# The query product leaves PSUM in one ScalarE copy, and its two parts are made from SBUF by VectorE and POOL

## The chip, the cores and the metric

The kernel runs on one core of one Trainium2 chip. The metric is the device time of one execution in microseconds (us). Before the change the median of three runs is 1530.5 us (1527.78 to 1530.98). A core has five engines that the text names: TensorE (PE in the profile; PEld are its weight loads), VectorE (DVE), ScalarE (ACT), GpSimd (POOL) and SyncE (SP, which here issues DMAs). SBUF is the working memory, and PSUM holds the results of TensorE.

## The reference

The model takes `x` of shape (4, 1024, 256) in float32 and adds four sublayers to it, each behind a layer norm: a linear recurrence over time, a feed-forward part with two top-32 gates, attention, and the feed-forward part again:

```
x = x + lru(layernorm(x));  x = x + ffn(layernorm(x))
x = x + attention(layernorm(x));  x = x + ffn(layernorm(x))
```

The attention has 8 heads of width 64 with a low-rank key and value path. All that matters here is this part of it:

```
q = (x @ Wq.T).reshape(b, t, 8, 64)
latent = x @ Wkv_down.T
k, v = latent @ Wk_up.T, latent @ Wv_up.T
out = softmax(q k^T / 8) v;   return out @ Wo.T
```

Everything is float32 in the reference. The kernel gets close to that by splitting a value into a high part, rounded to the type[...] (`F32R`), and a low part, the value minus its high part.

## The kernel before

**Tiling.** `x` stays in SBUF as 32 tiles of 128 tokens by 256 features, eight for each batch element. In attention the key weights are folded into the query weights (`wqk`, 256 by 512), so that scores are a product of a query with the 64-wide latent. The latent is kept transposed in two parts, `kh` (high) and `kl` (low), each laid down twice, on partitions 0 to 63 and 64 to 127.

**Queries.** `Attention.queries(b, nb, g)` (line 843) makes the queries of a pair of heads `g` (four pairs) for 512 tokens (`nb`, two for each batch element `b`): 32 calls in all. Six matmuls (`products`, line 170) fill a PSUM tile `pmq` of 128 partitions by 512: head 0 of the pair on partitions 0 to 63, head 1 on 64 to 127. The result is a tile `qs` of 128 by 2 by 512: for head `j`, one half of the partitions holds the high part and the other half the low part. The score product then multiplies high and low parts with the latent in one pass, as its contraction runs over all 128 partitions. Lines 852 and 853 make these parts for each `j`: ScalarE copies `pmq` to the half of `qs` named `mine`, rounding it; VectorE subtracts this from `pmq` and writes the half named `other`. So one `pmq` is read four times, twice by each engine. `qs` has two buffers.

**Heads.** `Attention.heads` (line 856) is the main stream. It walks over pairs of heads and query tiles of 128 tokens, and for each head it takes a step: four score matmuls into a PSUM tile `sc` (line 886, two buffers of two banks), the row maximum `nm` on VectorE (line 890), the exponential `pr` on ScalarE (line 894), and then one of two ways of transposing `pr`. Odd query tiles go over TensorE (`ptp`, line 905, copied by ScalarE at line 910). Even ones are cast to two half-precision parts `pd`, the high one on ScalarE (line 897) and the low one on POOL (line 898), and SyncE issues a transposing DMA (line 899). `values_sum` (line 921) multiplies with the latent (`pmo`, line 930), and transposes the reciprocal row sums (`rows`, made by POOL at line 926, line 938), which ScalarE copies to `rb` (line 940) and VectorE multiplies in (line 941). There are 256 steps.

**Side work and its order.** `merge` (line 962) interleaves the main stream with side work: each entry has the step at which it begins. Queries for pair `g` begin seven steps before its first score. The other entries are the output projection (`pmy`), the layer norms and transposes for the next batch element (`pt`, `pml`, `pv`), the head of the second feed-forward part (`pt`, `pc`) and 24 tiles of the first feed-forward part (`pl`, `px`, `pf`, with `ex`, `xg` and `full` behind them). All this side work and `values_sum` take their PSUM tiles in turn from two banks with the tag "s". The order in which the instructions stand on each engine's queue follows this program order, changed by a planner that plays the program through with its own durations (`schedule_with_timeline_sim=True`). On the chip each engine works through its queue in that order.

Of the kernel before, what the change touches and what calls it, by code (L numbers as in the profile page):

```python
# [10 lines left out]
F32 = mybir.dt.float32  # L11
# [5 lines left out]
ALU = mybir.AluOpType  # L17
# [4 lines left out]
P = 128  # L22
# [142 lines left out]
def products(nc, dst, pairs, start=True, stop=True):  # L165


    terms = [(x, y) for a, b in pairs for x, y in ((a[0], b[0]), (a[0], b[1]), (a[1], b[0]))]
    for i, (x, y) in enumerate(terms):
        nc.tensor.matmul(dst, x, y, start=start and i == 0, stop=stop and i == len(terms) - 1)  # L170
# [602 lines left out]
class Attention:  # L773
# [68 lines left out]
    def queries(self, b, nb, g, psum, tag):  # L842

        nc, xnt = self.nc, self.xnt[b, nb]
        qs = self.qs[b, nb, g] = self.wp.tile([P, 2, 512], F32R, tag="qs", name="qs", bufs=2)
        pm = psum.tile([P, 512], tag, "pmq")
        products(
            nc, pm, [([t[:, k, g * P : (g + 1) * P] for t in self.wqk], [t[:, k, :] for t in xnt]) for k in range(KD)]
        )
        for j in range(2):  # L850
            mine, other = slice(j * HD, (j + 1) * HD), slice((1 - j) * HD, (2 - j) * HD)
            nc.scalar.copy(qs[mine, j, :], pm[mine, :])
            nc.vector.tensor_tensor(qs[other, j, :], pm[mine, :], qs[mine, j, :].bitcast(F32), ALU.subtract)  # L853
        yield

    def heads(self, b, psum):
# [468 lines left out]
```

## Time and profile before

| what | value |
|---|---|
| median of the runs | 1530.5 us (1527.78 to 1530.98, three runs) |
| the profiled execution's own time | 1528.76 us |
| its span, first to last instruction | 1527.0 us |
| mean granted clock of TensorE | 0.946 |
| busy over the span: TensorE | 1286.5 us (84%) |
| weight loads | 955.6 us (63%) |
| VectorE | 1184.6 us (78%) |
| ScalarE | 1017.5 us (67%) |
| POOL | 680.3 us (45%) |
| `sc`, first to last start | 376.0 to 1292.0 us |

The profile shows one execution. A group is a set of instructions of one line, one engine and one shape, with its count, its busy time, and the idle time of its engine just before them with what ended it. "A <- B" in a list of waits reads: engine A was idle before that instruction until B was done. Engines overlap, so their busy times don't add up to the span; a wait costs time only where its engine sets the pace.

### The profile page before, as it was taken

How to read it: one execution, taken by the hardware profiler on the slowest of the kernel's cores; microseconds unless marked ns; L12 is line 12 of the kernel's file. 1: busy time of each engine (PE TensorE's matmuls, PEld its weight loads, DVE VectorE, ACT ScalarE, POOL GpSimd, SP SyncE). 2: the span in 40 equal slices, each digit the busy share in tenths (PEclk: the TensorE clock that was granted, in tenths of full speed). 3: DMA queues.
4: the chain of work that ended last, by engine and by line, in shares of the span. 5: the costliest groups of instructions: out<-in, count | busy, mean ns of one | idle time of the engine just before them, and what ended most of it. 6: DMA issues, size and time to landing. Idle time of an engine off the chain costs nothing. (4 is left out here: it accounts for less than half of the span.)

```text
span 1527.0 us, 28727 instructions
## 1 busy us (share of the span) xinstructions
PE 1286.5 (84%) x10134; PEld 955.6 (63%) x10136; DVE 1184.6 (78%) x3682; ACT 1017.5 (67%) x2152; POOL 680.3 (45%) x849
## 2 busy tenths in 40 slices
PE   4879998697898898888998989889999999566675
PEld 3535465376677766766776767677777777334454
DVE  8976665697868887878768687777676675599998
ACT  5353433566887877797777787877777776475674
POOL 2033332161545454544544554454344444067776
PEclk9999999698999999999999999999999999688899
DMA  3110000321454343434433445334344545000000
GB/s 118 32 41 15 21 21 21 128 97 49 84 93 90 61 77 73 77 70 82 82 74 60 72 79 86 61 61 83 68 82 79 92 86 96 1 15 24 22 25 28
DMA packets 288609, 96.51 MB, mean 63 GB/s; under 512 B 268233, under 2 KB 284626, under 8 KB 288466
## 3 DMA queue, kind: packets, MB, share of 16 engines
q1 hardware_dynamic: 283024, 88.50, 28.7%
q10 hardware_dynamic: 5442, 6.18, 1.2%
q8 instruction: 80, 1.31, 0.4%
q14 instruction: 63, 0.52, 0.1%
HBM read 16.01 MB, written 11.53 MB: 18 GB/s over the span
## 5 line engine op out<-in xcount | busy, mean ns | idle before, releaser
L898 POOL TENSOR_TENSOR pd<-pr,pd 128x1024 f16<-128x1024 f32 x128 | 273.5, 2141 | 247.6 <-ACT pd L897 185.7
L890 DVE TENSOR_REDUCE nm<-sc 128x1 f32<-128x1024 f32 x256 | 308.5, 1217 | 78.9 <-PE sc L886 77.5
L894 ACT ACTIVATE pr<-sc,nm 128x1024 f32<-128x1024 f32 x256 | 285.9, 1119 | 84.6 <-DVE nm L892 47.0
L886 PE MATMUL sc<-kh,qs 128*128 128x512 f32 x512 | 184.3, 438 | 26.4 <-ACT pr L894 18.8
L886 PE MATMUL sc<-kl,qs 128*128 128x512 f32 x512 | 162.0, 397 | 0.0
L674 DVE MATCH_REPLACE8 wk<-m,wk 128x256 f32<-128x256 f32 x384 | 154.9, 406 | 0.1
L910 ACT COPY p<-ptp 128x512 f32<-128x512 f32 x224 | 124.1, 590 | 45.3 <-PE ptp L905 33.7
L674 DVE MAX8 m<-wk 128x8 f32<-128x256 f32 x384 | 151.3, 412 | 0.4
L930 PE MATMUL pmo<-p,la 128*64 128x128 f32 x2048 | 144.0, 289 | 6.1 <-ACT ft L524 2.9
L905 PE MATMUL ptp<-ident,pr 128*128 128x128 f32 x1024 | 138.3, 275 | 12.9 <-ACT pr L894 12.4
L930 PEld LDWEIGHTS pmo<-p,la 128*64 128x64 f32 x2048 | 122.8, 144 | 25.0 <-ACT ft L524 5.1
L905 PEld LDWEIGHTS ptp<-ident,pr 128*128 128x128 f32 x1024 | 115.6, 140 | 34.8 <-ACT pr L894 22.2
L897 ACT CAST pd<-pr 128x1024 f16<-128x1024 f32 x128 | 133.5, 1054 | 5.6 <-DMA d<-pd 4.6
L886 PEld LDWEIGHTS sc<-kh,qs 128*128 128x128 f32 x512 | 85.2, 195 | 51.1 <-ACT pr L894 29.8
L886 PEld LDWEIGHTS sc<-kl,qs 128*128 128x128 f32 x512 | 97.0, 190 | 23.2 <-issue 1.4
L930 PE MATMUL pmo<-d,lb 128*64 128x128 f16 x3072 | 103.4, 222 | 7.6 <-DVE qs L853 2.6
L930 PEld LDWEIGHTS <-lb 128*64 128x64 f16 x3072 | 92.2, 111 | 26.3 <-issue 20.1
L628 POOL TENSOR_TENSOR ex<-ex,wk 128x512 f32<-128x512 f32 x61 | 77.6, 1273 | 57.4 <-DVE wk L674 45.5
L926 POOL COPY rows<-rs 128x128 f32<-128x128 f32 x128 | 36.1, 294 | 124.4 <-PE pmo L938 76.3
L941 DVE TENSOR_TENSOR on<-pmo,rb 128x128 f32<-128x128 f32 x128 | 36.4, 285 | 66.8 <-ACT rb L940 66.3
L147 PE MATMUL pt<-ident,xn 128*128 128x128 f32 x256 | 47.8, 309 | 44.5 <-ACT xn L145 32.9
L699 PE MATMUL pf<-wf,vt 128*128 128x256 f32 x288 | 81.2, 427 | 4.6 <-ACT vt L697 4.2
(307 smaller groups left out, 2768.6 us busy)
## 6 DMA issues: line engine op xcount, KB each, us to landing
tt<-ft SPq DMA_DIRECT2D x16, 256.0 KB
tt<-tt SPq DMA_DIRECT2D x8, 512.0 KB
out<-x SPq DMA_DIRECT2D x32, 128.0 KB
x<-in_x ACTq DMA_DIRECT2D x6, 512.0 KB
pf<-pfs SPq DMA_DIRECT2D x12, 256.0 KB
full<-pf SPq DMA_DIRECT2D x24, 128.0 KB
d<-pd SPq DMA_TRANSPOSE x128
wa<-in_w_attn SPq DMA_DIRECT2D x2, 640.0 KB
```

Source lines behind the costliest of these rows:

```text
L147: nc.tensor.transpose(pt[:, k, i * P : (i + 1) * P], xn[:, k * P : (k + 1) * P], ident)
L628: pool.tensor_tensor(ex, ex, wk, ALU.subtract)
L674: ins = make(*args).ins
L699: nc.tensor.matmul(dst, vt[:, k, :], w.wf[:, k, :], start=(k == 0 and bias is None), stop=(k == KD - 1))
L886: nc.tensor.matmul(sc[:, sl], qs[:, j, q * P : (q + 1) * P], kk[:, sl], start=(i == 0), stop=(i == 1))
L890: nc.vector.tensor_reduce(nm, sc, AX.X, ALU.max, negate=True)
L894: nc.scalar.activation(pr, sc, AF.Exp, bias=nm, accum_out=ssum[:, j : j + 1])
L897: nc.scalar.copy(pd[:, 0, :], pr)
L898: nc.gpsimd.tensor_tensor(pd[:, 1, :], pr, pd[:, 0, :], ALU.subtract)
L905: nc.tensor.transpose(pt[:, kk, :], pr[:, kc * P : (kc + 1) * P], self.ident)
L910: nc.scalar.copy(dst, pt)
L930: nc.tensor.matmul(po[j * HD : (j + 1) * HD, 0, :], v, pts[j][:, c, :], start=(n == 0), stop=(n == len(terms) - 1),)
```

## The change

The product is first copied whole, from PSUM to a new SBUF tile `q` of 128 by 512 (one buffer), by one ScalarE instruction. For each head, VectorE then copies `mine` from `q` to `qs`, rounding it, and POOL subtracts that from `q` into the half `other`. So `pmq` is read once, by one engine; both inputs of the subtraction are now in SBUF.

```diff
         products(
             nc, pm, [([t[:, k, g * P : (g + 1) * P] for t in self.wqk], [t[:, k, :] for t in xnt]) for k in range(KD)]
         )
+        q = self.wp.tile([P, 512], F32, tag="q", name="q")
+        nc.scalar.copy(q, pm)
         for j in range(2):
             mine, other = slice(j * HD, (j + 1) * HD), slice((1 - j) * HD, (2 - j) * HD)
-            nc.scalar.copy(qs[mine, j, :], pm[mine, :])
-            nc.vector.tensor_tensor(qs[other, j, :], pm[mine, :], qs[mine, j, :].bitcast(F32), ALU.subtract)
+            nc.vector.tensor_copy(qs[mine, j, :], q[mine, :])
+            nc.gpsimd.tensor_tensor(qs[other, j, :], q[mine, :], qs[mine, j, :].bitcast(F32), ALU.subtract)
         yield
```

## The prediction

> **What bounds the kernel now.** I first read busy time by stretch, to find the stretch that the change lies in. All 64 copies and all 64 subtractions of the query product start between 366 and 1256 us, that is in the attention stage, so the sums below are about this stretch.
>
> ```profile
> core 0: us, PE busy (x) PEld busy (x) DVE busy (x) ACT busy (x) POOL busy (x), PEclk, DMA share, GB/s
> 366.00:376.00 10.00, 7.74 (x36) 6.17 (x35) 5.04 (x17) 4.85 (x11) 1.09 (x2) 0.66 0.00 0
> 376.00:1292.00 916.00, 822.39 (x8245) 655.14 (x8246) 687.13 (x1714) 700.90 (x1366) 428.76 (x420) 0.98 0.42 77
> ```
>
> In these 916 us TensorE is busy for 822 (90%), ACT for 77%, DVE for 75%, POOL for 47%. TensorE sets the pace, and its matmuls are not changed; what can be won or lost is its 94 us of idle time. The waits of TensorE in that window say what the idle time is made of (engine and line, what it waited for, us in total, times, longest):
>
> ```profile
> PE sc L886 <- ACT pr L894: 18.8, 22, 2.8
> PE ptp L905 <- ACT pr L894: 12.4, 16, 1.8
> PE pt L147 <- DVE qs L853: 9.0, 5, 2.1
> PE sc L886 <- DVE qs L853: 6.7, 7, 1.7
> PE pmo L930 <- DVE qs L853: 4.4, 5, 1.6
> ...
> PE pmy L170 <- DVE qs L853: 2.6, 2, 1.3
> ```
>
> Two different waits end with the query's subtraction (L853). `sc` reads `qs`: 6.7 us in 7 waits are true data waits. `pt`, `pmo` and `pmy` read no query at all; they want a PSUM bank. All side work shares the two banks tagged "s", and `pmq` holds one until the last of its four readers is done. That is 9.0 + 4.4 + 2.6 = 16.0 us in 12 waits. One such place in the timeline of ACT and DVE:
>
> ```profile
> 686.02 0.59 ACT L852 CAST qs<-pmq 64x512 fp32r<-64x512 f32 x1
> ...
> 687.33 0.68 DVE L853 TENSOR_TENSOR qs<-pmq,qs 64x512 fp32r<-64x512 f32 x1
> ...
> 688.05 0.58 ACT L852 CAST qs<-pmq 64x512 fp32r<-64x512 f32 x1 [0.86 <-DVE qs L853]
> ...
> 689.22 0.69 DVE L853 TENSOR_TENSOR qs<-pmq,qs 64x512 fp32r<-64x512 f32 x1
> ```
>
> The four readers of the one bank take turns (the second cast sits idle for 0.86 us behind the first subtraction). This product began at 682.59 and left its bank at 689.91, so it held it for 7.3 us. Read the same way for all 32 queries, the hold is 4.9 to 11.1 us, mean 7.8, of which the product itself is about 1.6 and the wait of the first cast for ACT 0.8.
>
> **The change, step by step.** The durations come from these rows of the groups, the first three in the same window, L269 in the set-up at 30 to 60 us (count, busy us, mean ns), and from the view of one line, L636 (min/median/max ns):
>
> ```profile
> L910 ACT COPY p<-ptp 128x512 f32<-128x512 f32 x221 | 122.3, 590 | 41.1 <-PE ptp L905 33.0 <-PE pmo L930 7.3
> L953 POOL TENSOR_TENSOR onp<-on,onp 128x512 fp32r<-128x512 f32 x28 | 35.9, 1280 | 20.3 <-ACT onp L952 16.3 <-DVE m L674 3.1 <-PE ptp L905 0.9
> L908 DVE COPY p<-ptp 128x512 f32<-128x512 f32 x29 | 19.8, 683 | 5.3 <-PE ptp L905 5.0 <-PE pmo L930 0.2
> L269 DVE TENSOR_SCALAR t<-st,cs_s 128x256 f32<-128x256 f32 x1 | 0.3, 339 | 0.0
> ```
>
> ```profile
> L636 DVE SCALAR_TENSOR_TENSOR full<-full,rs,ex x24: 474/864/2319, 402.1 to 1063.7; 128x256 f32<-128x256 f32 x24
> ```
>
> *ACT.* Removed: 64 casts at 0.58 = 37.1 us. Added: 32 copies of 128x512 out of PSUM at 0.59 (L910, the same shape and path) = 18.9. ACT gains 18.2 us.
>
> *DVE.* Removed: 64 subtractions at 0.689 = 44.1 us. Added: 64 copies of 64x512 from SBUF to SBUF. No such row exists. Upper end: L908, 0.68 (it reads PSUM). Lower end: L269 is a one-input float32 pass inside SBUF, 339 ns for 256 columns against 272 for 128, so 0.52 ns per column, and 339 + 256 x 0.52 = 0.47 us for 512. I take 0.45, since the new copy has no per-partition scalar to fetch: 29 us. This rate has a price. L636, a DVE instruction with its inputs in SBUF, takes 0.474 us at best and 2.319 at worst; the worst began at 788.56, while a POOL subtraction of `pd` ran from 788.47 for 2.13 us. The Trainium skill, "SBUF — State Buffer", section "Who interferes with whom", gives the rule, and it speaks against this change: a DVE copy at the double rate takes the port pair that it shares with GpSimd, and whichever issues second is blocked for the whole of the other's instruction. The old subtraction never paid this (0.683 to 0.694 in all 64), as one of its inputs was PSUM. POOL runs 47% of the time, and the remainder of a running POOL instruction, weighted by length, is about 0.8 us (the 2.14 us `pd` dominates), so the rule adds some 0.4 us to each copy: 0.85. By the uncontended row DVE gains 64 x (0.69 - 0.45) = 15 us, by the rule it loses 64 x 0.16 = 10. I take the loss, since L636's median of 864 ns shows the blocking is common here.
>
> *POOL.* Added: 64 subtractions of 64x512. L953 gives 1.28 for 128x512; fewer partitions save nothing (L1035, 32x256, took 0.664, and L659, 128x256, 0.729). What no row shows is that this one writes the other half of the partitions; from 1.28 to twice that, I take 1.28: 82 us, POOL from 47% to 56%.
>
> Now what reaches TensorE:
>
> 1. *The bank.* `pmq` is freed after the one copy: 1.6 + 0.8 + 0.6 = 3.0 us instead of 7.8. The 12 bank waits have a mean of 1.3 us, well under the 4.8 won, so this cause goes; but the other bank or an `xn` of ACT may be next. I take 60% of 16.0: **-10 us** (bounds 0 and -16).
> 2. *The scores.* From the end of the product the shortest chain to the first score was 0.58 + 0.69 = 1.27; it becomes 0.59 + 0.45 + 1.28 = 2.3, so +1.0. This is hidden wherever the first score comes later. In 25 of the 32 queries both subtractions were done 1.6 to 18.7 us before the first score; the first score of the other 7 starts right at the first subtraction's end (688.07 in the query above). If nothing else moves that is 7 x 1.0 = +7. But the queries are late there because the side work ahead of them is held up in the two banks, which step 1 eases. I take **+3** (bounds -6.7, all these waits gone, and +25: 7 x (1.0 + 0.4 + 2.14), each behind a whole `pd` on POOL).
> 3. *ACT's load* falls by 18.2 of 916 us, 2.0 points of its 23 idle ones. Waits of TensorE for ACT are 31 us in the two rows shown and about 44 with the smaller ones; in that proportion (9%) **-4**.
> 4. *DVE's load* rises by 10 us, 1.1 points of 25. It acts mainly through `nm`, for which ACT waits 47.0 + 26.2 us: **+2** by the rule. By the uncontended row alone it would be -2, and the sum below 4 us lower.
> 5. *POOL's queue.* Behind the new subtractions wait `pd` (its DMA result is used several scores later), `ex`, and `rows` (L926), which TensorE transposes at the end of each value sum. By the timeline nine of the 128 `rows` copies are ready less than 1.4 us before that transpose (median 6.2). At a 9% chance (82 of 916 us) of meeting a new subtraction: 9 x 0.09 x 1.3 = **+1**.
>
> The sum is -10 + 3 - 4 + 2 + 1 = -8 us against the profiled execution, which took 1528.8 (span 1527.0 and 1.8 around it): 1521. The three runs shown have a median of 1530.5, 1.7 above it; the same -8 gives 1522.5 there, and between the two I say **1522**.
>
> Nothing covers the new buffer `q`, which has one slot, but the products start at least 12.9 us apart, and the last reader is done some 4 us after the copy.
>
> **The rivals.**
>
> *A. The longer chain decides (slower).* Place: the first scores of 7 queries, which have no slack. Price: up to 3.5 us each. The planner may put the POOL subtractions behind a `pd` that itself waits for ACT (POOL waited 185.7 us for those casts, up to 8.9 at a time), and TensorE, which runs in order, then stands. Gains elsewhere are about 11 net, so it decides from 1.5 us per query; at the full price 1521 - 3 + 25 = 1543. For it: the wait is already there with no slack. Against it: POOL was idle at the moment the new subtraction would start in all 7.
>
> *B. The bank waits only change their name (same).* The 16 us go to the next-late cause and step 1 gives 0: with -4, +3, +2, +1 the result is 1531 to 1532. For it: `pt <- ACT`, `pf <- DVE nm` and others of 1 to 5 us are in the same list. Against it: 4.8 us is large beside a mean wait of 1.3.
>
> *C. The written order comes out worse (slower).* The order on each queue is made by a planner from its own timing of the program, and the start offsets of the side work (6.75, 48.25, -5.5 scores) suit the present order. Batches 1 and 2 repeat each other's slack to 0.01 us in six of eight queries, so a bad place is paid more than once. A score step is 916/256 = 3.6 us; one lost step in each of four batches is 14 us: 1536.
>
> **How the numbers follow.** The forecast has 0.47, A 0.22, B 0.15, C 0.16. About 0.2% (3 us, from 1527.4 to 1533.6) is what a measurement of this kernel can tell from no change. Faster is the forecast alone, 0.47; same is B, 0.15; slower is A and C, 0.38. The likeliest case's own range is 1514 to 1528. The range over all starts where the full 16 us, half of the 6.7 and the 4 are won and steps 4 and 5 cost nothing (16 + 3.4 + 4 = 23, and 1529 - 23 = 1506) and ends at A's full price, **1506 to 1545**.
>
> **What would show it.** In the new profile: no TensorE wait of `pt`, `pmo` or `pmy` on `qs`, and the bank held about 3 us (step 1); `sc` waiting on POOL `qs` for under 10 us in all (step 2; over 20 is A); DVE copies spread from about 0.4 to 2.5 us (the blocking; all at one value means none); POOL subtractions near 1.28; ACT's busy time down by 18. TensorE idle time from other causes grown by as much as `qs` lost is B; many groups of waits changed that have nothing to do with queries is C. The forecast is wrong if the stage's idle time of TensorE, 94 us, doesn't fall.

## The result, and the profile after

The change makes the kernel slightly slower. In 21 runs of each on one chip the median goes from 1528.03 us to 1533.54 us, a ratio of **1.0033 [1.0023, 1.0042]**; a second comparison on another chip gave 1.0030 [1.0019, 1.0041]. The forecast was 1522, faster. The measured time lies within the forecast's range, but the sign is wrong. The profiled execution took 1530.07 us, span 1528.4 us, mean granted clock 0.938.

Busy time of the engines by stretch, kernel after:

```profile
core 0: us, PE busy (x) PEld busy (x) DVE busy (x) ACT busy (x) POOL busy (x), PEclk, DMA share, GB/s
376.00:1292.00 916.00, 822.35 (x8260) 653.63 (x8260) 696.02 (x1718) 682.54 (x1339) 513.46 (x483) 0.98 0.44 78
```

The loads moved as the change says: ACT 700.9 to 682.5, POOL 428.8 to 513.5, DVE 687.1 to 696.0. TensorE is busy as before, 822 of 916 us. So the 94 us of idle time that the forecast wanted to shorten are still there (916.0 less 822.4). The waits of TensorE in the same window, kernel after (engine and line, what it waited for, us in total, times, longest), say what became of them:

```profile
PE ptp L907 <- ACT pr L896: 17.8, 20, 1.8
PE sc L888 <- ACT pr L896: 17.2, 24, 2.2
PE pmq L170 <- DVE on L943: 8.9, 4, 2.3
PE pmo L932 <- DVE on L943: 7.0, 7, 1.9
...
PE pmy L170 <- POOL onp L955: 3.7, 4, 1.0
PE pmo L932 <- ACT q L851: 3.5, 6, 0.9
...
PE pt L147 <- DVE on L943: 3.1, 2, 1.6
...
PE sc L888 <- POOL qs L855: 1.7, 2, 0.8
```

No `pt`, `pmo` or `pmy` waits on `qs` any more: the 16.0 us of bank waits behind the subtraction are gone. Of waits on the query's bank 3.5 us are left, now behind the copy `q` itself. In place of the rest stand waits on `on` (L943, L941 before), the last reader of `pmo`, which holds the other of the two "s" banks. They were 3.9 us before, in four rows of which these are the largest,

```profile
PE pmy L170 <- DVE on L941: 1.5, 1, 1.5
PE pt L147 <- DVE on L941: 1.3, 1, 1.3
```

and are 20.7 us now (the three rows shown and three small ones of 0.9, 0.6 and 0.2): 16.8 came for the 16.0 that went. The second profile of the kernel after has 20.8 us of them, and the kernel with `q` in another pool, below, has 21.1 (the second profile of the kernel before has 3.9).

One such place, among those where the new copies take part. These are lines of the timeline of the kernel after (start, us, engine, instruction, idle time before it and what ended it), around the product that the prediction followed at 682.59 in the kernel before:

```profile
682.45 1.64 PE L170 MATMUL pmq<-xnt,wqk 128*128 128x512 f32 x6
...
687.47 0.62 ACT L851 COPY q<-pmq 128x512 f32<-128x512 f32 x1
...
687.74 2.14 POOL L900 TENSOR_TENSOR pd<-pr,pd 128x1024 f16<-128x1024 f32 x1 [0.64 <-POOL rows L928]
688.14 1.97 PE L932 MATMUL pmo<-p,la 128*64 128x128 f32 x32 [0.33 <-ACT q L851]
688.72 1.90 DVE L854 CAST qs<-q 64x512 fp32r<-64x512 f32 x2
689.53 0.30 ACT L942 COPY rb<-pmo 128x128 f32<-128x128 f32 x1
...
691.84 0.27 DVE L943 TENSOR_TENSOR on<-pmo,rb 128x128 f32<-128x128 f32 x1
692.16 1.53 PE L932 MATMUL pmo<-d,lb 128*64 128x128 f16 x48 [1.79 <-DVE on L943]
```

`pmq` leaves its bank at 688.1 and the next `pmo` follows at once. The one after that needs the other bank. Its `rb` is there at 689.83, but `on` starts only at 691.84, since DVE's queue holds the two query copies and parts of a top-32 gate ahead of it. The two copies take 1.90 us instead of two times 0.40: the first of them started while a POOL `pd` was running and ended just after it. TensorE stands for 1.79 us.

But query copies stand between `rb` and `on` in only four of the 17 waits, 3.9 of the 20.7 us. The five longest, 10.9 us together, are of another kind. One of them, kernel after:

```profile
701.55 4.22 POOL L900 TENSOR_TENSOR pd<-pr,pd 128x1024 f16<-128x1024 f32 x2 [5.03 <-ACT pd L899]
701.57 2.13 DVE L64 SCALAR_TENSOR_TENSOR ax_t<-ax_rs 128x4 f32<-128x4 f32 x1
...
703.74 2.05 DVE L65 TENSOR_TENSOR ax_t<-ax_t,ax_v 128x4 f32<-128x4 f32 x1
...
706.30 0.28 DVE L943 TENSOR_TENSOR on<-pmo,rb 128x128 f32<-128x128 f32 x1
...
706.63 1.65 PE L170 MATMUL pmq<-xnt,wqk 128*128 128x512 f32 x3 [2.23 <-DVE on L943]
```

Here `rb` is ready at 702.58. Ahead of `on` on DVE's queue stand tiny operations of a layer norm, `ax`, which take 0.16 us elsewhere. Two of them start within 0.1 us of the start of a POOL `pd` and take as long as that does. At the same layer norm in the kernel before, `on` stands right behind the first such operation, only one `pd` runs (2.13 us from 701.93), and TensorE does not wait:

```profile
701.96 2.12 DVE L64 SCALAR_TENSOR_TENSOR ax_t<-ax_rs 128x4 f32<-128x4 f32 x1
...
704.01 0.28 DVE L941 TENSOR_TENSOR on<-pmo,rb 128x128 f32<-128x128 f32 x1
```

So most of the waits on `on` come from where the written order puts `on` and `pd`, not from the length of the new copies. That order came with the moved work: with the unused tile alone, below, these waits are 3.7 us. No run moved `on` alone, so what another place for it would give is not shown.

The new operations, from the view of each line, kernel after (ns min/median/max, first and last start):

```profile
L851 ACT COPY q<-pmq x32: 574/586/644, 368.4 to 1249.4; 128x512 f32<-128x512 f32 x32
L854 DVE CAST qs<-q x64: 398/424/2255, 369.0 to 1251.3; 64x512 fp32r<-64x512 f32 x64
L855 POOL TENSOR_TENSOR qs<-q,qs x64: 1258/1310/1461, 370.2 to 1253.0; 64x512 fp32r<-64x512 f32 x64
L636 DVE SCALAR_TENSOR_TENSOR full<-full,rs,ex x24: 476/1060/2431, 404.1 to 1059.1; 128x256 f32<-128x256 f32 x24
```

What is left to explain is the 0.33%. I cut every profile at two places: the end of the last convolution of the first feed-forward part (when ScalarE has read it, 292.6 us in the kernel before), and the first and last score (start of the first, end of the last). "Idle" is the stage's length less TensorE's busy time.

| kernel | convolution to first score | first to last score | of it TensorE idle | last score to end |
|---|---|---|---|---|
| before | 83.5 | 916.4 | 93.6 | 234.6 |
| before, second profile | 83.3 | 914.2 | 92.7 | 236.3 |
| after | 86.9 | 912.3 | 92.5 | 236.9 |
| after, second profile | 87.3 | 917.3 | 93.4 | 235.8 |

Idle time in the attention stage is unchanged. About 3.7 us were lost before the first score, in the mean of two, where only the first query or two had run. The last stretch is about 0.9 us longer in the mean of two, within what the two profiles of one kernel differ by.

### The profile page after: what moved, and what is told of

The parts are those of the page before. It is cut to its first block, busy times and chain, and to the rows that moved or that the text cites. A ratio compares the mean times of both kernels' runs of the same rounds, so it can differ in the third digit from the quotient of the medians.

```text
span 1528.4 us, 28806 instructions
## 1 busy us (share of the span) xinstructions
PE 1291.6 (85%) x10136; PEld 955.6 (63%) x10136; DVE 1194.6 (78%) x3682; ACT 996.0 (65%) x2120; POOL 766.9 (50%) x913
## 4 chain that ended last, share of the span: by engine, by line
PE 43%; DVE 34%; ACT 11%; issue 5%; POOL 4%; DMA 2%; ACTq 0%; POOLq 0%; DVEq 0%
PE pmo L932 8%; PE sc L888 8%; DVE wk L674 7%; DVE nm L892 6%; DVE m L674 5%; PE ptp L907 4%; ACT pr L896 4%; PE po L437 3%; PE pu L170 2%; PE pl L556 2%; PE pmy L170 2%; PE pz L452 1%; DMA d<-pd 1%; PE pfa L567 1%; PE pt L147 1%
## 5 line engine op out<-in xcount | busy, mean ns | idle before, releaser
L932 PE MATMUL pmo<-p,la 128*64 128x128 f32 x2048 | 137.4, 277 | 5.0 <-DVE x L961 1.7
L932 PEld LDWEIGHTS pmo<-p,la 128*64 128x64 f32 x2048 | 115.0, 137 | 26.0 <-issue 7.1
L855 POOL TENSOR_TENSOR qs<-q,qs 64x512 fp32r<-64x512 f32 x64 | 86.6, 1352 | 64.3 <-DVE qs L854 61.5
L699 PE MATMUL pf<-wf,vt 128*128 128x256 f32 x288 | 85.2, 439 | 4.2 <-ACT vt L697 3.7
L556 PE MATMUL pl<-lint,xc_f 128*128 128x512 f32 x128 | 73.3, 660 | 9.8 <-ACT xc_f L587 9.8
```

What stands on the lines that cost most here:

```text
L556: self.last_logits = nc.tensor.matmul(v, x, w.lint, start=False, stop=True).ins
L699: nc.tensor.matmul(dst, vt[:, k, :], w.wf[:, k, :], start=(k == 0 and bias is None), stop=(k == KD - 1))
L855: nc.gpsimd.tensor_tensor(qs[other, j, :], q[mine, :], qs[mine, j, :].bitcast(F32), ALU.subtract)
L932: nc.tensor.matmul(po[j * HD : (j + 1) * HD, 0, :], v, pts[j][:, c, :], start=(n == 0), stop=(n == len(terms) - 1),)
```

## The experiments

### The tile alone

The kernel before with nothing but the allocation of `q`; the tile is never used.

```diff
+        self.wp.tile([P, 512], F32, tag="q", name="q")
```

> The kernel before, with only the tile q allocated and never used: no instruction is added or moved by hand, but the addresses of the attention's tiles shift by 2 KB and the planner writes another order from the end of the first stage on. If the slowdown of 0.33% is the new order that comes with the tile's place: ratio to before 1.002 to 1.005, first score near 379 us instead of 376. If it is the moved work itself: 0.999 to 1.001.

Measured: **1.0032 [1.0021, 1.0043]**, as much as the change loses, without any of its work. The stretch from the convolution to the first score takes 86.1 us. The traces show how an unused tile can do this: the order of the instructions differs from that of before on every engine, from 273 us on for VectorE and from 303 us on for TensorE, and in the attention stage too. (The two profiles of the kernel before have the same order on every engine.) One visible part is the load of the attention weights, `wa`, the view of one tile, first in the kernel before and then with the unused tile:

```profile
L712 SPq DMA_DIRECT2D wa<-in_w_attn x2: 424/726/1029, 294.4 to 294.9; - x2
```

```profile
L712 SPq DMA_DIRECT2D wa<-in_w_attn x2: 430/430/431, 268.5 to 269.0; - x2
```

It is issued 26 us earlier. What is lost before the first score is lost at one place some 60 us after that. Timeline of TensorE and ACT in the kernel before:

```profile
345.30 3.64 ACT L587 ACTIVATE xc_f<-xc_f,bt,bs 128x512 f32<-128x512 f32 x5
348.84 0.45 ACT L650 ACTIVATE ob<-pf,rs 128x256 f32<-128x256 f32 x1
349.19 0.80 ACT L587 ACTIVATE xc_f<-xc_f,bt,bs 128x512 f32<-128x512 f32 x1
349.34 1.99 PE L567 MATMUL pfa<-wf,tt 128*128 128x256 f32 x8 [2.04 <-ACT ob L650]
...
352.78 1.13 PE L567 MATMUL pf<-wf,tt 128*128 128x256 f32 x4 [1.45 <-ACT pfs L581]
354.08 1.03 PE L699 MATMUL pf<-wf,vt 128*128 128x256 f32 x4
```

And with the unused tile:

```profile
348.41 4.34 ACT L587 ACTIVATE xc_f<-xc_f,bt,bs 128x512 f32<-128x512 f32 x6
354.16 1.05 ACT L581 COPY pfs<-pfa 128x512 f32<-128x512 f32 x2
354.78 2.07 PE L567 MATMUL pf<-wf,tt 128*128 128x256 f32 x4 [5.81 <-ACT pfs L581]
356.86 1.91 PE L699 MATMUL pf<-wf,vt 128*128 128x256 f32 x4
356.89 0.47 ACT L650 ACTIVATE ob<-pf,rs 128x256 f32<-128x256 f32 x1
```

Before, a short `ob` stood ahead of the last of six activations on ACT's queue and freed a bank for eight matmuls. Now all six run in one row, followed by a table load, and TensorE waits 5.81 us in one piece instead of 2.04 and 1.45. After that wait the same two groups of four matmuls take 2.07 and 1.91 us instead of 1.13 and 1.03. The windows of the two kernels give the reason, columns as in the first fence, before and then with the tile:

```profile
352.70:356.60 3.90, 3.82 (x19) 3.36 (x20) 3.79 (x16) 2.23 (x6) 1.46 (x2) 1.00 0.35 134
```

```profile
354.70:358.60 3.90, 3.82 (x10) 2.81 (x11) 3.83 (x18) 2.67 (x7) 1.08 (x2) 0.50 0.35 134
```

The granted clock is 0.50 instead of 1.00: in 3.9 us ten matmul records were done instead of 19. The Trainium skill, "TensorE: Matmul & The Clock Gate", Part 1, says that an idle window of about 3.4 us brings TensorE down to half rate; the trace agrees here, where TensorE did nothing in the 3.4 us before the clock fell (350.1 to 353.5). But so long a wait is not needed. In the profile of the last changed kernel below (offset 48.75, `q` in its own pool) the wait of 2.04 us at the same place is followed by half rate, with TensorE busy for 1.36 of the 3.4 us before; columns as above:

```profile
348.70:352.10 3.40, 1.36 (x7) 0.89 (x6) 3.40 (x15) 3.40 (x6) 2.10 (x3) 1.00 0.00 0
352.10:355.50 3.40, 2.77 (x7) 1.76 (x6) 3.40 (x15) 2.88 (x6) 1.26 (x2) 0.51 0.04 16
```

With the unused tile the wait costs 2.3 us more and the half clock 1.8 us more, 4.1 in all, of which 2.7 are left at the first score of this run. All six profiles of kernels with a 2 KB tile in the working pool show this wait of 5.81 us, followed by the two groups at 2.07 to 2.08 and 1.91 us. None of the other twelve has it.

That is not the whole loss of about 4.9 us. In this one profile the stage from the first to the last score is longer too, 921.5 us, with the same idle time (93.3) but 48.2 us at half rate, where the two profiles of the kernel before have 37.5 and 34.3. This execution took 1539.02 us, against a median of 1535.18 for this kernel, so how much of that is usual is not known.

### The change with its tile elsewhere

The whole change, with `q` taken from a pool of its own that is opened ahead of the first feed-forward part.

```diff
+    qpool = ctx.enter_context(tc.tile_pool(name="q_own", bufs=1))
...
+        at.qp = qpool
...
-        q = self.wp.tile([P, 512], F32, tag="q", name="q")
+        q = self.qp.tile([P, 512], F32, tag="q", name="q")
```

> The change, with q in a pool of its own that is opened ahead of the first stage, so that all later tiles shift alike; allocating it there without using it leaves every queue's order as it was before. If the tile's place costs the 0.33%: ratio to before 0.995 to 0.999, as the attention stage itself was 4 us shorter from first to last score in the changed kernel's profile. If the moved work costs it: 1.002 to 1.005, as with the change as made.

Measured: **0.9964 [0.9950, 0.9979]**, faster than before. The convolution-to-score stretch is 82.5 us, with the waits of 2.04 and 1.45 us in it as before. This kernel and the kernel after were then measured once more, on another chip and side by side.

> The change with q in a pool of its own ahead of the first stage, a second time and beside the changed kernel. If the moved work gains in this order: ratio to before 0.995 to 0.998 again, first score near 376 us. If the first result was the chip or chance: 0.999 to 1.002.

> The changed kernel as it is, on the same chip as the next three. If the tile's place and the new order that follows from it cost what the first experiments showed: ratio to before 1.002 to 1.005, and the first score of its profile at 379 us or later.

Measured: 0.9972 [0.9957, 0.9987] and 1.0030 [1.0019, 1.0041]. Where `q` lies is worth 0.6% (1.0030 / 0.9972 = 1.0058) with the same arithmetic on the same engines. Between the two profiles, whose spans differ by 7.0 us, 5.8 lie before the first score (87.3 against 81.5) and 2.2 after the last (235.8 against 233.6); the stage is alike (917.3 and 916.7).

The kernel before was also profiled a second time, to have a measure of how far two profiles of one kernel differ.

> The kernel before, for a second profile of it: first score near 376 us, first to last score 914 to 920 us. A first score at 379 us or later would take the place of the tile out of the explanation.

Measured: 0.9997 [0.9985, 1.0008]; the stage took 914.2 us where it had taken 916.4, with idle times of 92.7 and 93.6.

### Address or order?

An unused tile of half the size at the same place: it moves the addresses of what is allocated after it, but the order of the instructions in the trace is that of before on every engine.

```diff
+        self.wp.tile([P, 256], F32, tag="pad", name="pad")
```

> The kernel before with an unused tile of 1 KB per partition at the place where the change allocates q (half of q's size). It moves the addresses of what is allocated after it, but the order written on every queue stays that of before, instruction for instruction. Theory 'it is the order that the tile redraws which costs': 0.999 to 1.001, first score at 375 to 379 us and about 83 us from the last f1 convolution to the first score. Rival 'the shifted addresses cost by themselves': 1.002 to 1.004 and 86 to 87 us.

Measured: **0.9992 [0.9981, 1.0002]**, 83.8 us to the first score, and `wa` issued at 293.2. Addresses shifted by 1 KB cost nothing, so the loss goes with the order that came with the 2 KB tile; a shift by 2 KB in the old order was not run. Why the planner writes another order for 2 KB and the same for 1 KB is not settled here.

### Is the stage's gain or loss one of a single order?

Two offsets of the side work were moved, to get other written orders of the attention stage. First 6.75 scores for each tile of the first feed-forward part became 6.5, in the kernel before, in the change with `q` in its own pool, and in the change as it is:

```diff
-            start = 1 + 6.75 * n if n < TPB else STEPS * (n // TPB) - STEPS + 48.25 + 8 * (n % TPB + 1)
+            start = 1 + 6.5 * n if n < TPB else STEPS * (n // TPB) - STEPS + 48.25 + 8 * (n % TPB + 1)
```

> The kernel before with the tiles of the first feed-forward part begun every 6.5 steps of the main stream instead of 6.75: the same work, the same addresses, another order from step 20 or so on. As a measure of what an order alone is worth: between 0.997 and 1.006 of before; more likely slower, as 6.75 suits the present order.

> The change with q in its own pool, and 6.5 steps as in o1_b. If the moved work itself gains, whatever the order: 0.2 to 0.6% faster than o1_b. If e4's gain was a lucky order: within 0.1% of o1_b or slower than it.

> The changed kernel, q in the working pool, with the side work's start at 6.5 scores per tile where it was 6.75: the same tile at the same place, the attention stage in another order. Theory 'the loss sits ahead of the first score and the moved work gains little or nothing in the stage': the stretch from the last f1 convolution to the first score is again 86 to 87 us (81.7 with q in its own pool at this offset, 82.9 without q), and the ratio is that of the run with q outside (0.998) plus 0.002 to 0.004: 1.000 to 1.003. Rival 'the loss was an accident of one attention order': 0.997 to 0.999.

Measured: 1.0010 [0.9997, 1.0023], 0.9984 [0.9974, 0.9994] and 1.0022 [1.0012, 1.0032]. With the tile in its own pool the moved work gains 0.26% (0.9984 / 1.0010 = 0.9974); with it in the working pool the stretch before the first score is 87.6 us again, against 81.7, and the gain is lost.

Then the other offset, 48.25, became 48.75, before and with `q` in its own pool.

```diff
-            start = 1 + 6.75 * n if n < TPB else STEPS * (n // TPB) - STEPS + 48.25 + 8 * (n % TPB + 1)
+            start = 1 + 6.75 * n if n < TPB else STEPS * (n // TPB) - STEPS + 48.75 + 8 * (n % TPB + 1)
```

> The kernel before with the offset 48.25 of the later side work at 48.75: another written order of the attention stage, without the change. It is the base for the next run. Either theory: 0.998 to 1.005.

> The change with q in a pool of its own ahead of the first stage, with the same offset at 48.75. Theory 'the moved work is worth 0.2 to 0.4% in any order if the tile stays out of the working pool': 0.996 to 0.998 of the run before it. Rival 'the gain of the two earlier pairs belonged to their orders': 0.999 to 1.003 of it.

Measured: 0.9994 [0.9984, 1.0004] and **0.9933 [0.9915, 0.9951]**: 0.6% between them, more than either theory expected, and the fastest kernel of the study (median 1519.91, six runs). The stage from the first to the last score, in the windows of the two, columns as above, first without and then with the change:

```profile
375.50:1291.80 916.30, 820.39 (x8247) 654.60 (x8248) 688.65 (x1714) 701.03 (x1367) 428.73 (x421) 0.98 0.43 77
```

```profile
378.10:1282.60 904.50, 813.64 (x8245) 646.96 (x8246) 692.26 (x1714) 681.04 (x1335) 513.06 (x482) 0.99 0.45 79
```

Of the 11.8 us, 5.0 are idle time of TensorE (95.9 to 90.9) and 6.8 its busy time: the same matmuls ran faster, since the clock's records show 17.1 us at half rate in the stage instead of 33.9. The waits on `on`, from the list of TensorE's waits of the changed one, are smaller than in the kernel after but still there:

```profile
PE pmq L170 <- DVE on L943: 6.7, 3, 2.3
PE pmo L932 <- DVE on L943: 4.6, 4, 1.8
...
PE pt L147 <- DVE on L943: 3.1, 2, 1.5
```

So with `q` in its own pool the moved work is faster by 0.3% to 0.6% in three written orders. Only in the third do the profiles find the gain in the stage. In the first pair the stage takes 915.8 and 916.7 us with the change, 916.4 and 914.2 without; in the second 916.3 against 916.7. Where those gains lie is not shown, and the waits on `on` are there in all three (21.1, 19.7 and 16.5 us). In the order of the change as it was made the work gains nothing: 1.0033 and 1.0030 stand against 1.0032 for the tile alone.

### Which engine makes which part

Five more kernels free the bank with the one copy, and differ in who makes the high and low parts from `q`. Two have `q` in the working pool.

Low parts on VectorE:

```diff
-            nc.gpsimd.tensor_tensor(qs[other, j, :], q[mine, :], qs[mine, j, :].bitcast(F32), ALU.subtract)
+            nc.vector.tensor_tensor(qs[other, j, :], q[mine, :], qs[mine, j, :].bitcast(F32), ALU.subtract)
```

> The change, with the low parts on VectorE from SBUF and nothing new on POOL. If POOL's 64 new subtractions (82 us) cost the time (longer chain, queue, shared port): 0.997 to 1.000, faster than the change. If VectorE's load does (44 us of subtractions come back beside 27 us of copies, VectorE then near 79% in the stage): 1.005 or more. If it is the order alone: anything from 0.998 to 1.005, with no relation to POOL.

High parts on ScalarE:

```diff
-            nc.vector.tensor_copy(qs[mine, j, :], q[mine, :])
+            nc.scalar.copy(qs[mine, j, :], q[mine, :])
```

> The change, with the high parts made by ScalarE from SBUF, so that VectorE has nothing of the query at all and ScalarE copies three times. If VectorE's copies on the shared port cost the time: 0.997 to 1.000. If ScalarE's load matters more (37 us of casts come back beside 19 us of copies): 1.004 or more. If it is the order alone: anything from 0.998 to 1.005.

Measured: 1.0211 [1.0190, 1.0231] and 1.0001 [0.9992, 1.0010]. The other three have `q` in its own pool: low parts on VectorE, high parts on ScalarE, and both of these edits at once.

> q in its own pool; high and low parts both on VectorE from SBUF, nothing on POOL. If the 2.1% of the second experiment was VectorE's load (27 us added, 37 taken off ScalarE, port waits on the subtractions): 1.012 to 1.022 here too. If it was the tile's place: 0.998 to 1.004.

> q in its own pool; the high parts by ScalarE, the low parts by POOL, nothing on VectorE. If VectorE is what counts in this stage (44 us taken off it): 0.993 to 0.996, faster than the change with q in its own pool. If ScalarE is (19 us added to it, where the change takes 18 off): 0.998 to 1.002.

> q in its own pool ahead of the first stage; one ScalarE copy out of PSUM as in the change, then the high parts by ScalarE and the low parts by VectorE, both from q: the engines of before, 19 us of copies more on ScalarE, nothing on POOL. If freeing the bank after one copy is what gains: ratio to before 0.996 to 0.999. If the gain is VectorE's and ScalarE's relief: 1.001 to 1.006, since ScalarE has more to do.

Measured: 1.0300 [1.0286, 1.0315], 1.0051 [1.0038, 1.0064] and 1.0147 [1.0121, 1.0173]. All three are slower than either theory expected. From first to last score, all with `q` in its own pool:

| high / low parts by | stage, us | ACT busy | DVE busy | POOL busy | TensorE idle |
|---|---|---|---|---|---|
| (kernel before) | 916.4 | 701.3 | 687.4 | 429.1 | 93.6 |
| DVE / POOL (the change) | 915.8 | 682.3 | 696.3 | 513.0 | 92.1 |
| ACT / POOL | 922.3 | 715.3 | 648.5 | 508.2 | 91.9 |
| ACT / DVE | 929.7 | 718.0 | 691.7 | 435.9 | 101.8 |
| DVE / DVE | 957.8 | 683.8 | 725.3 | 434.5 | 116.5 |

The row ACT / DVE is the nearest test of step 1: the same two engines make the same two parts as before, and the bank is freed early, for one more ACT copy per query (ACT +16.7, DVE +4.3). The stage gets 13.3 us longer, in the fastest of the five runs. In TensorE's waits of this kernel no side work waits on `qs`, 1.5 us are left behind the copy `q`, the waits on `on` are 13.5 us, and those for the exponential, which held 31.2 us before, hold 49.0:

```profile
PE sc L888 <- ACT pr L896: 25.9, 32, 2.9
PE ptp L907 <- ACT pr L896: 23.1, 29, 2.3
```

The bank's early release and ACT's added copy can't be told apart in it, and its written order is another one again. In the row DVE / DVE, 38 us more of DVE go with a stage that is 41 us longer. Here the subtraction has both inputs in SBUF, and its spread, from the view of its line, is as wide as the copies' (before, with one input in PSUM, all 64 took 0.683 to 0.694 us):

```profile
L855 DVE TENSOR_TENSOR qs<-q,qs x64: 684/687/2684, 372.4 to 1297.0; 64x512 fp32r<-64x512 f32 x64
```

The working pool is not the worse place for every kernel: DVE / DVE takes 1.0211 with `q` there and 1.0300 outside, and ACT / POOL 1.0001 and 1.0051. The stretch before the first score is longer in both with the tile there (85.0 against 84.3, and 86.9 against 83.2), but the stage is 10.8 and 6.9 us shorter. The tile's place chooses an order; whether that is a good one for the stage has to be measured.

## Why the prediction was wrong

**Step 1, the bank (-10, bounds 0 and -16): this failed.** Its first half holds: the bank is held 3.35 us on average (3.0 expected, 7.8 before), and no side work waits on `qs`. The failed sentence is "this cause goes; but the other bank or an `xn` of ACT may be next. I take 60%". The other bank was next for all of it, 16.8 us on `on` for 16.0 on `qs`. The step gave 0, as in rival B, whose likelihood I had put at 0.15. The mean wait of 1.3 us against 4.8 won was the wrong comparison: side work takes the two banks in turn, so the slack of the other bank's holder had to be compared. `on` waits on DVE, for 3.9 of the 20.7 us behind the copies that the change puts there, and for 10.9 behind operations of a layer norm that last as long as a `pd` on POOL.

**Step 2, the scores (+3, bounds -6.7 and +25).** Better than forecast: true data waits of `sc` on the query fall from 6.7 us in 7 to 1.7 us in 2 waits. The chain got longer (4.5 us on average from the product's end to the first low part, 2.8 before), but the queries came earlier: from the product's start to the first score it is 7.7 us at the least, 4.6 before. Rival A falls.

**Step 3, ACT's load (-4).** The load fell by 20.1 us in the stage (18.2 expected), but TensorE's waits for `pr` rose, 31.2 to 35.0 us. (All its waits for ACT were 48 us before, not 44, which changes the step by less than half a us.) They are not in proportion to ACT's load: `pr` waits for `nm` on DVE. The waits of ACT, kernel after:

```profile
ACT pr L896 <- DVE nm L894: 52.5, 39, 4.2
ACT pr L896 <- DVE nm L892: 39.9, 32, 5.9
```

These held 47.0 and 26.2 us before: ACT's load fell by 20 us, and these waits for DVE grew by 19.

**Step 4, DVE's load (+10 us of load, +2 of time).** The load rose by 7.2 us in the stage, near the value by the rule on the shared port and far from the -15 by the uncontended row. But that is luck: it rose in other instructions than the step said. The copies have a mean of 0.55 us, not 0.85: only 7 of 64 took over 0.75, and 56 ran within 0.45. Their busy time is 34.2 us for 42.7 of subtractions, a gain of 8.5 in the window. What took it back is other DVE work: L636, whose mean went from 972 to 1279 ns (+7.4), and the 18 tiny `ax_t` operations of 128x4 on L65, 3.4 to 13.3 us (+9.9). Five of these 18 take 2.05 us, each beside a `pd` on POOL; one takes 1.14 beside a new subtraction. Of L636, nine take over 1.5 us now and four did before, beside `pd` or `onp` and never beside a new subtraction. So what these met was, but for one, not the added POOL work but old POOL work that the new order puts beside them. The runs show the times, not what they waited for. The price of +2 for this load, together with step 3's -4, was of the wrong sign: +3.8 us in the waits for `pr`.

**Step 5, POOL's queue (+1).** The subtraction takes 1.35 us on average (1.28 expected; writing the other half of the partitions costs nothing that is seen), POOL's load rose by 84 us (82 expected), and no wait of TensorE on `rows` appeared. A small one did on `onp`, 3.7 us in 4 waits.

**The buffer.** "Nothing covers the new buffer `q`, which has one slot" asked only whether the slot is free in time. This is the step that the sum lacked, and it holds the sign: the allocation alone costs 0.32%, about 4.9 us, of which 2.7 are found before the first score in its one profile. Rival C had the mechanism, a written order that comes out worse, at 0.16, and priced it at a lost score step in each of four batches, 14 us. The one place found sits in front of the attention stage, where C did not look.

**The sum.** -8 us was forecast. With the tile in its own pool, the moved work measured -4 to -5 us in the first two pairs and -9 in the third. So a gain of about the expected size exists in some written orders. But I cannot credit it to my steps: the first two pairs show none of it in the stage, and in the kernel as changed TensorE's idle time of the stage went from 93.6 to 92.5 us and from 92.7 to 93.4 in the second profiles, and the forecast named exactly this as its test ("wrong if the stage's idle time of TensorE, 94 us, doesn't fall").

## What to carry to other kernels

Before a freed buffer is booked as a gain, ask who holds the next buffer of its ring and what that release is queued behind; freeing one of two banks early won nothing here, since the other bank's release came late on VectorE's queue, behind a little of the new work and more of the old. Where a planner writes the order, a new tile is a change in itself: try the allocation alone, and compare the queues instruction by instruction, before the work is judged. And move work by which engine releases the critical one, not by how busy an engine is: 20 us taken from ScalarE bought nothing here, and the waits of its main instruction for VectorE grew by 19.

## What the runs showed of the hardware

A slower run of one kernel shows a lower granted clock, more or less closely. In four groups of runs of the kernel before, 17 to 62 each, the mean clock of a run (about 0.94) and its time correlate with -0.58 to -0.79, and 0.01 of clock goes with 4.5 to 9.8 us; for the other kernels with 14 runs or more the correlation is -0.33 to -0.84. Which of the two moves the other is not shown by this. Kernels differ in it, too: with the offset of 6.5 and `q` in its own pool TensorE's idle time in the stage fell from 95.0 to 88.3 us, but 54.6 us of the stage ran at half rate instead of 44.9, and the stage was only 0.4 us shorter (916.7 to 916.3).

The traces say more on what sets the clock in the stage, where the longest wait of TensorE is 2.8 us before and 2.3 after. The clock's records change in steps of 3.41 us, between full and half rate. Over the 18 profiles the clock falls to half 165 times between the first and the last score. In the 3.41 us just before, TensorE was busy for 41% in the median, and for less than half in 134 of the 165. Where the clock was full and stayed full, 4451 times, TensorE was busy for less than half of the 3.41 us before in only 47. One such fall in the kernel before, columns as above:

```profile
836.83:840.24 3.41, 0.99 (x7) 0.78 (x8) 3.33 (x10) 3.16 (x5) 2.12 (x1) 1.00 0.00 0
840.24:843.66 3.42, 3.27 (x15) 2.04 (x15) 2.43 (x6) 3.06 (x6) 2.17 (x3) 0.50 0.79 150
```

So several short waits that fall into one such stretch go with half rate as a long one does. The other 31 falls stay open, and so does how much of the 0.6% of the last pair would hold in another order.

A VectorE copy of 64x512 from SBUF to SBUF with rounding takes 0.40 to 0.43 us in 56 of 64 cases and up to 2.26 us beside a `pd` on POOL. Of the two POOL subtractions of a query, the first starts while the second copy still runs (in 31 of 32 queries) and takes 1.43 us on average (1.32 to 1.46); the second, beside no copy, takes 1.28 (1.26 to 1.30).
